# Score products of one attention layer, spread over four quarters of the array instead of two

## The chip, the core and the metric

The kernel runs on one core of a Trainium2 chip. The metric is the device time of one execution in microseconds; lower is better. The kernel before takes 2292.18 us, the median of three runs (2292.06 to 2292.21).

## What is computed

Four graph layers are applied to x, 128 graphs of 64 nodes with 256 features each. Each layer is added to its input: `x = x + layer(relu(layernorm(x)))`. Layer 0 is a graph convolution with LSTMs over windows, layer 2 a graph attention, layer 3 a filter in the eigenbasis of the graph. The change concerns the attention of layer 1, cut here to its middle part (N = 64 nodes, H = 4 heads of hd = 64 features):

```python
q = (x1 @ Wq).reshape(B, N, H, hd).transpose(0, 2, 1, 3)
k = (x1 @ Wk).reshape(B, N, H, hd).transpose(0, 2, 1, 3)
v = (x1 @ Wv).reshape(B, N, H, hd).transpose(0, 2, 1, 3)
scores = jnp.einsum('bhnd,bhmd->bhnm', q, k) / np.sqrt(hd)
scores = jnp.where(adjacency[None, None] > 0, scores, -1000000000.0)
attn = jax.nn.softmax(scores, axis=-1)
o = jnp.einsum('bhnm,bhmd->bhnd', attn, v)
o = o.transpose(0, 2, 1, 3).reshape(B, N, D)
o = o @ Wo + bo
x2 = _layernorm(x1 + o, g2, be2)
# ... the feed-forward part and a last layer norm follow
```

Everything is fp32. A graph and a head give one 64x64 score matrix, a product over 64 features.

## The kernel before

The 128 graphs are cut into 16 half groups of 8 graphs, or HT = 4 tiles of 128 rows (two graphs in a tile). `q` and `k` are kept with features on the partitions: `qT[:, m, :]` holds feature block m (128 features, so heads 2m and 2m+1, the first on partitions 0-63 and the second on partitions 64-127), and the free dimension runs over the 512 nodes of the half group. `bat(b)` is the 64 columns of graph b, `tok(t)` the 128 columns of tile t.

```python
        ps = [bank("qk") for m in range(2)]
        with plan.burst():
            for par, m, b in [(r, r ^ f, b) for f in range(2) for b in range(2 * HT) for r in (f, 1 - f)]:
                r = slice(par * N, par * N + N)
                PE.matmul(ps[m][r, bat(b)], qT[r, m, bat(b)], kT[r, m, bat(b)], start=True, stop=True)
        s = tm(4 * HT, N)
        for m in range(2):
            sm = s[:, m * 2 * HT:(m + 1) * 2 * HT, :]
            V.scalar_tensor_tensor(sm, ps[m].rearrange("p (b k) -> p b k", k=N), 0.125, vec(mask1, 2 * HT), op0=ALU.mult, op1=ALU.add)
            stat = plan.value("stat")
            softmax_shift(sm, stat[:, :2 * HT])
            ACT.activation(sm, sm, AF.Exp)
            # ... sum, reciprocal (VectorE), product with the reciprocal (GpSimd)

        pT = fm()
        for m in range(2):
            evac(pT[:, m, :], transposes([flat(s[:, (m * HT + t) * 2:(m * HT + t) * 2 + 2, :]) for t in range(HT)]), m)
        oT = fm()

        po = [bank("o") for half in range(2)]
        with plan.burst():
            for m, t, half, par in [(m, t, half, par) for m in range(2) for t in range(HT) for half in range(2) for par in range(2)]:
                r = slice(half * N, half * N + N)
                PE.matmul(po[half][par * N:par * N + N, bat(m * HT + t)], v[r, t, bat(2 * m + par)], pT[r, m, bat(2 * t + par)], start=True, stop=True)
```

The first operand of `PE.matmul` is the output in PSUM, the second the stationary operand, the third the moving one. Which partitions the operands lie on fixes the rows of the array that a product uses, and which partitions the output lies on fixes its columns. A product of 64 by 64 takes a quarter of the 128x128 array. In the score loop the output half equals the row half (`ps[m][r, ...]`, `qT[r, ...]`), and the two banks alternate from one product to the next: with f = 0 the pairs are (low rows, bank 0) and (high rows, bank 1), with f = 1 (high rows, bank 0) and (low rows, bank 1). In the second loop (attention times V, `po`) row half and output half are independent.

The instructions are not issued as they are written: a layer in the kernel records them and chooses the order on each engine beforehand from costs that it assumes. A burst counts there as one operation:

```python
    @contextmanager
    def burst(self):
        self.run, self.whole = None, True
        yield
        self.run.cost = 0.3 + 0.036 * len(self.run.calls)
        self.run.lat = self.run.cost + 0.22
        self.run, self.whole = None, False
```

All instructions are issued from one line (331), so the profile is read by operations, shapes and tile names; tile names are those of the pool buffer that happened to be free.

Of the kernel before, what the change touches and what calls it, by code (L numbers as in the profile page):

```python
# [12 lines left out]
N = 64  # L13
# [856 lines left out]
HT = 4  # L870
# [41 lines left out]
def gnn_kernel(ctx: ExitStack, tc: tile.TileContext, a, out):  # L912
# [46 lines left out]
    PE, V, ACT, G, SP = (plan.proxy(e) for e in ("PE", "V", "ACT", "G", "SP"))  # L959

    def bank(name):
        return plan.value("bank")
# [156 lines left out]
    bat = lambda b: slice(b * N, (b + 1) * N)  # L1119

    def tm(n=HT, f=D):

        return plan.value("big")[:, :n * f].rearrange("p (t f) -> p t f", f=f)

    def fm():

        return plan.value("big")[:, :2 * HT * P].rearrange("p (c n) -> p c n", c=2)
# [4 lines left out]
    def transposes(srcs):  # L1132

        pt = bank("tr")
        for i, s in enumerate(srcs):
            PE.transpose(pt[:, i * P:(i + 1) * P], s, ident)
        return pt
# [158 lines left out]
    def evac(dst, src, i):  # L1296
        if i % 2:
            ACT.copy(dst, src)
        else:
            V.tensor_copy(dst, src)  # L1300

    def to_fm(src):

        dst = fm()
        for c in range(2):
            evac(dst[:, c, :], transposes([src[:, t, tok(c)] for t in range(HT)]), 1)
        return dst

    def proj_fm(w, src, m):
        ps = bank("fm")  # L1310
        for c in range(2):
            PE.matmul(ps, w[:, c, tok(m)], src[:, c, :], start=c == 0, stop=c == 1)
        return ps

    def proj_tm(lhs, w, nk, t0):

        ps = bank("tm")
        for t in range(2):
            for c in range(nk):
                PE.matmul(ps[:, t * D:(t + 1) * D], lhs(c, t0 + t), w[:, c, :], start=c == 0, stop=c == nk - 1)  # L1320
        return ps

    def pair(t, t0):
        return flat(t[:, t0:t0 + 2, :])

    def norm(t):

        sc, bi = ln_stats(t)
        for i in range(HT):
            ACT.activation(t[:, i, :], t[:, i, :], AF.Identity, scale=sc(i), bias=bi(i))  # L1330

    def softmax_shift(s, mx):

        V.reduce_max(mx, s, axis=AX.X)
        V.tensor_sub(s, s, mx.unsqueeze(2).to_broadcast(list(s.shape)))

    def relu_norm(x):
        sc, bi = ln_stats(x)
        h = tm()
        for t in range(HT):  # L1340
            ACT.activation(h[:, t, :], x[:, t, :], AF.Relu, scale=sc(t), bias=bi(t))
        return h

    def mix_fm(h, m):

        dst = fm()
        for c in range(2):
            ps = bank("mix")
            for t in range(HT):
                PE.matmul(ps[:, tok(t)], h[:, t, tok(c)], m(t), start=True, stop=True)  # L1350
            evac(dst[:, c, :], ps, 1)
        return dst

    def layer1(x):
        h = relu_norm(x)
        lx = mix_fm(h, lambda t: lapb)
        x1 = tm()
        for t0 in (0, 2):
            ps = proj_tm(lambda c, t: lx[:, c, tok(t)], Wc, 2, t0)
            V.tensor_add(x1[:, t0:t0 + 2, :], ps.rearrange("p (t f) -> p t f", t=2), vec(bc, 2))  # L1360
        norm(x1)
        for t0 in (0, 2):
            xp, hp = x1[:, t0:t0 + 2, :], h[:, t0:t0 + 2, :]
            V.tensor_mul(xp, xp, vec(g1, 2))
            G.tensor_add(xp, xp, vec(be1, 2))
            V.scalar_tensor_tensor(xp, xp, 0.0, hp, op0=ALU.max, op1=ALU.add)
        x1T = to_fm(x1)
        qT, kT, v = fm(), fm(), tm()
        for m in range(2):
            evac(qT[:, m, :], proj_fm(Wq, x1T, m), 0)  # L1370
            evac(kT[:, m, :], proj_fm(Wk, x1T, m), 1)
        for t0 in (0, 2):
            evac(pair(v, t0), proj_tm(lambda c, t: x1T[:, c, tok(t)], Wv, 2, t0), 1)
        for t0 in (0, 2):
            G.tensor_add(x1[:, t0:t0 + 2, :], x1[:, t0:t0 + 2, :], vec(bo, 2))

        ps = [bank("qk") for m in range(2)]
        with plan.burst():  # L1380
            for par, m, b in [(r, r ^ f, b) for f in range(2) for b in range(2 * HT) for r in (f, 1 - f)]:
                r = slice(par * N, par * N + N)
                PE.matmul(ps[m][r, bat(b)], qT[r, m, bat(b)], kT[r, m, bat(b)], start=True, stop=True)
        s = tm(4 * HT, N)
        for m in range(2):
            sm = s[:, m * 2 * HT:(m + 1) * 2 * HT, :]
# [4 lines that stand above are left out]
            ssum = stat[:, 2 * HT:4 * HT]  # L1391
            V.reduce_sum(ssum, sm, axis=AX.X)
            V.reciprocal(ssum, ssum)
            G.tensor_mul(sm, sm, ssum.unsqueeze(2).to_broadcast([P, 2 * HT, N]))

        pT = fm()
        for m in range(2):
            evac(pT[:, m, :], transposes([flat(s[:, (m * HT + t) * 2:(m * HT + t) * 2 + 2, :]) for t in range(HT)]), m)
        oT = fm()

        po = [bank("o") for half in range(2)]
        with plan.burst():
            for m, t, half, par in [(m, t, half, par) for m in range(2) for t in range(HT) for half in range(2) for par in range(2)]:
                r = slice(half * N, half * N + N)
                PE.matmul(po[half][par * N:par * N + N, bat(m * HT + t)], v[r, t, bat(2 * m + par)], pT[r, m, bat(2 * t + par)], start=True, stop=True)
        for half in range(2):
            evac(oT.rearrange("p c (t b n) -> p c t b n", t=HT, b=2)[:, :, :, half, :], po[half].rearrange("p (c t n) -> p c t n", c=2, t=HT), half)
        x2 = tm()
        for t0 in (0, 2):
            ps = proj_tm(lambda c, t: oT[:, c, tok(t)], Wo, 2, t0)  # L1410
            V.tensor_add(x2[:, t0:t0 + 2, :], ps.rearrange("p (t f) -> p t f", t=2), x1[:, t0:t0 + 2, :])
        norm(x2)
        x2T = fm()
        for c in range(2):
            ACT.activation(x2T[:, c, :], transposes([x2[:, t, tok(c)] for t in range(HT)]), AF.Identity, scale=g2c[:, c:c + 1], bias=be2c[:, c:c + 1])
        V.tensor_mul(x2, x2, vec(g2))
        for t0 in (0, 2):
            G.tensor_add(x2[:, t0:t0 + 2, :], x2[:, t0:t0 + 2, :], vec(b2, 2))
        mT = [fm() for i in range(2)]
        for m in range(4):  # L1420
            ACT.activation(mT[m // 2][:, m % 2, :], proj_fm(W1, x2T, m), AF.Gelu, bias=b1[:, m:m + 1])
        for t0 in (0, 2):
            ps = proj_tm(lambda c, t: mT[c // 2][:, c % 2, tok(t)], W2, 4, t0)
            V.tensor_add(pair(x2, t0), ps, pair(x2, t0))
        for t0 in (0, 2):
            G.tensor_add(x[:, t0:t0 + 2, :], x[:, t0:t0 + 2, :], vec(be3, 2))
        norm(x2)
        for t0 in (0, 2):
            V.tensor_mul(x2[:, t0:t0 + 2, :], x2[:, t0:t0 + 2, :], vec(g3, 2))
            V.tensor_add(x[:, t0:t0 + 2, :], x[:, t0:t0 + 2, :], x2[:, t0:t0 + 2, :])  # L1430
# [55 lines left out]
    for i, g in enumerate(ORDER):  # L1486
        plan.group = REST + 2 * i
        x = X[g]
        if g < len(put):
            x = load(back[g], put[g])  # L1490
        for h in range(GT // HT):
            plan.group = REST + 2 * i + h
            xh = x[:, h * HT:(h + 1) * HT, :]
            layer1(xh)
            layer2(xh)
            layer3(xh)
            SP.dma_start(xout[g * GT // HT + h], xh)
# [54 lines left out]
```

## Time and profile before

| | before |
|---|---|
| median time | 2292.18 us (2292.06 to 2292.21) |
| span of the profiled execution | 2291.3 us |
| TensorE busy, matmul records | 2254.4 us, 11288 |
| VectorE, ScalarE, GpSimd busy | 1693.3, 969.8, 565.7 us |
| granted TensorE clock, mean | 0.996 |

In the profile PE is TensorE's products, PEld its weight loads, DVE VectorE, ACT ScalarE, POOL GpSimd. Each fp32 product leaves two matmul records. A line of the timeline merges records of the same operation that follow each other: it shows the start of the first, the time to the end of the last, and how many there are. The ends of products overlap with the next products' starts, so the distance from one line's start to the next line's start is the better measure of what a burst costs TensorE. The groups of 64x64 products all have the form 64*64 64x64, whatever buffers they use:

```profile
L331 PE MATMUL bank<-big,big 64*64 64x64 f32 x384 | 9.7, 220 | 0.0
L331 PE MATMUL bank<-big,arena 64*64 64x64 f32 x320 | 7.6, 220 | 0.0
L331 PE MATMUL bank<-x,arena 64*64 64x64 f32 x256 | 7.5, 220 | 0.0
```

These three are the largest of sixteen such groups of layer 1; the columns are count, busy time in us, mean duration of one record in ns, and idle time before.

### The profile page before, as it was taken

What the parts mean: (1) busy time and instruction counts of PE and PEld (TensorE: products, weight loads), DVE (VectorE), ACT (ScalarE), POOL (GpSimd) and SP (SyncE); (2) the same over time, 40 slices, a digit from 0 to 9 for tenths busy, and PEclk for the clock granted to TensorE, in tenths of its full rate; (3) what the DMA queues carried; (4) which work ended last, traced back from release to release, by engine and by line L of the source; (5) the groups of instructions that cost most, each with busy time, mean ns of one, the idle gap of its engine ahead of it and who ended that gap; (6) DMA issues with size and microseconds to landing.
All of it is one profiled execution on the core that took longest, in us unless ns stands there. A gap on an engine that the chain in (4) does not pass through costs nothing.

```text
span 2291.3 us, 33480 instructions
## 1 busy us (share of the span) xinstructions
PE 2254.4 (98%) x11288; PEld 1595.1 (70%) x11288; DVE 1693.3 (74%) x6942; ACT 969.8 (42%) x1909; POOL 565.7 (25%) x856
## 2 busy tenths in 40 slices
PE   8999999999999999999999999999999999999997
PEld 5578478468568568568568558778777776876786
DVE  6656666566899999999988723767786867767775
ACT  3333333333333333333333443455564545555672
POOL 3101001101100100100100203535374535555342
PEclk9999999999999999999999999999999999999998
DMA  7000001000000000000000011000000000000001
GB/s 247 1 1 19 0 1 38 19 1 1 1 1 1 1 1 1 1 1 1 5 1 1 9 36 31 1 1 10 20 10 10 10 28 10 28 10 1 2 19 37
DMA packets 27405, 35.48 MB, mean 15 GB/s; under 512 B 3297, under 2 KB 24673, under 8 KB 26721
## 3 DMA queue, kind: packets, MB, share of 16 engines
q1 hardware_dynamic: 26128, 32.29, 4.2%
q8 instruction: 89, 1.46, 0.3%
q10 hardware_dynamic: 1104, 1.05, 0.2%
q14 instruction: 84, 0.68, 0.1%
HBM read 22.85 MB, written 10.49 MB: 15 GB/s over the span
## 4 chain that ended last, share of the span: by engine, by line
PE 91%; DVE 5%; ACT 2%; POOL 1%; issue 1%; DMA 0%; SPq 0%; DVEq 0%; ACTq 0%
PE bank L331 91%; DVE arena L331 2%; DVE big L331 1%; DVE stat L331 1%; DVE x L331 1%; POOL stat L331 1%; ACT big L331 1%; DVE mids L331 0%; ACT arena L331 0%; ACT L331 0%; ACT mids L331 0%; ACT Wih L331 0%; DMA adj<-in_adj_dram 0%; ACT x L331 0%; DVE Whh L331 0%
## 5 line engine op out<-in xcount | busy, mean ns | idle before, releaser
L331 PE MATMUL bank<-big,Wih 128*128 128x512 f32 (+2 forms) x2640 | 887.6, 478 | 2.2 <-DVE arena L331 1.1
L331 PEld LDWEIGHTS bank<-big,Wih 128*128 128x128 f32 x2640 | 490.0, 190 | 275.3 <-issue 172.4
L331 ACT ACTIVATE mids<-bank,bl 128x256 f32<-128x256 f32 (+2 forms) x624 | 345.2, 563 | 637.0 <-PE bank L331 622.3
L331 PE MATMUL bank<-big,Whh 128*128 128x256 f32 (+3 forms) x1640 | 507.3, 444 | 0.0
L331 DVE TENSOR_TENSOR arena<-arena 64x21 f32<-64x21 f32 (+6 forms) x2316 | 375.9, 193 | 34.7 <-POOL arena L331 1.8
L331 PEld LDWEIGHTS bank<-big,Whh 128*128 128x128 f32 x1640 | 306.4, 190 | 132.4 <-issue 65.5
L331 POOL TENSOR_SCALAR stat<-stat 128x4 f32<-128x4 f32 (+1 forms) x228 | 67.5, 297 | 722.4 <-DVE stat L331 709.7
L331 DVE TENSOR_TENSOR big<-big,mids 128x256 f32<-128x256 f32 (+2 forms) x192 | 93.8, 489 | 123.7 <-ACT mids L331 122.3
L331 DVE TENSOR_TENSOR big<-mids 128x512 f32<-128x512 f32 (+2 forms) x256 | 145.9, 574 | 47.0 <-ACT mids L331 43.5
L331 ACT ACTIVATE mids<-big 128x256 f32<-128x256 f32 (+2 forms) x176 | 89.8, 510 | 99.6 <-DVE big L331 64.8
L331 PE MATMUL bank<-Wih,big 128*128 128x256 f32 (+1 forms) x560 | 130.2, 365 | 0.2 <-ACT big L331 0.2
L331 DVE TENSOR_SCALAR arena<-arena 64x1 f32<-64x1 f32 (+4 forms) x598 | 120.3, 210 | 8.2
L331 POOL TENSOR_TENSOR arena<-arena 64x1 f32<-64x1 f32 x66 | 43.6, 661 | 322.6 <-ACT arena L331 170.2
L331 POOL TENSOR_TENSOR stat<-stat,mhalf 128x4 f32<-128x4 f32 (+1 forms) x114 | 120.4, 1057 | 6.5
L331 PEld LDWEIGHTS bank<-Wih,big 128*128 128x128 f32 x560 | 97.6, 190 | 21.9 <-issue 10.7
L331 PE MATMUL bank<-Whh,big 128*128 128x256 f32 (+2 forms) x512 | 110.2, 358 | 1.4 <-DVE x L331 1.0
L331 ACT COPY big<-bank 128x512 f32<-128x512 f32 x113 | 63.0, 587 | 111.5 <-PE bank L331 94.1
L331 PEld LDWEIGHTS bank<-Whh,big 128*128 128x128 f32 (+1 forms) x512 | 82.3, 183 | 21.9 <-issue 8.3
L331 DVE COPY arena<-bank 64x1 f32<-64x1 f32 (+24 forms) x190 | 41.2, 220 | 71.4 <-PE bank L331 64.9
L331 PEld LDWEIGHTS bank<-adjTb,mids 128*128 128x128 f32 x512 | 69.8, 193 | 25.7 <-issue 17.0
L331 DVE BATCH_NORM_STATS2 stat<-x 128x6 f32<-128x256 f32 x240 | 87.2, 410 | 0.1
L331 ACT ACTIVATE mids<-x,stat 128x256 f32<-128x256 f32 x92 | 48.4, 591 | 88.2 <-POOL stat L331 88.2
(334 smaller groups left out, 3313.1 us busy)
## 6 DMA issues: line engine op xcount, KB each, us to landing
x<-in_x_dram SPq DMA_DIRECT2D x7, 1024.0 KB, 13.2
out_dram<-x SPq DMA_DIRECT2D x12, 512.0 KB, 2.9
Wih<-in_WihT_dram SPq DMA_DIRECT2D x3, 1024.0 KB, 15.7
Whh<-in_WhhT_dram SPq DMA_DIRECT2D x3, 1024.0 KB, 12.2
put<-x SPq DMA_DIRECT2D x2, 1024.0 KB, 4.4
arena<-put SPq DMA_DIRECT2D x2, 1024.0 KB, 5.9
out_dram<-arena SPq DMA_DIRECT2D x4, 512.0 KB, 3.0
Whh<-in_W_dram SPq DMA_DIRECT2D x2, 512.0 KB, 3.8
```

The source lines that it names most:

```text
L331: getattr(self.engines[op.eng], name)(*map(real, args), **{k: real(a) for k, a in kw.items()})
```

## The change

The heads of the second feature block (m = 1) write their scores to the other 64 partitions: output half `r ^ m` instead of `r`. With that the four products of a graph (two blocks by two heads) use each quarter of the array once, and the loop runs through them in turn. Everything behind it sees the two heads of block 1 on swapped partition halves; the attention-times-V loop undoes this by reading the other 64 columns of `pT`. The aim is that four products can be under way in the array where two were.

```diff
         ps = [bank("qk") for m in range(2)]
+        half = lambda i: slice(i * N, i * N + N)
         with plan.burst():
-            for par, m, b in [(r, r ^ f, b) for f in range(2) for b in range(2 * HT) for r in (f, 1 - f)]:
-                r = slice(par * N, par * N + N)
-                PE.matmul(ps[m][r, bat(b)], qT[r, m, bat(b)], kT[r, m, bat(b)], start=True, stop=True)
+            for b, m, r in [(b, m, r) for b in range(2 * HT) for m in range(2) for r in range(2)]:
+                PE.matmul(ps[m][half(r ^ m), bat(b)], qT[half(r), m, bat(b)], kT[half(r), m, bat(b)], start=True, stop=True)
...
-        po = [bank("o") for half in range(2)]
+        po = [bank("o") for i in range(2)]
         with plan.burst():
-            for m, t, half, par in [(m, t, half, par) for m in range(2) for t in range(HT) for half in range(2) for par in range(2)]:
-                r = slice(half * N, half * N + N)
-                PE.matmul(po[half][par * N:par * N + N, bat(m * HT + t)], v[r, t, bat(2 * m + par)], pT[r, m, bat(2 * t + par)], start=True, stop=True)
+            for m, t, i, r in [(m, t, i, r) for m in range(2) for t in range(HT) for i in range(2) for r in range(2)]:
+                PE.matmul(po[i][half(r), bat(m * HT + t)], v[half(i), t, bat(2 * m + r)], pT[half(i), m, bat(2 * t + (r ^ m))], start=True, stop=True)
```

More of the change, by code (lines that the diff above doesn't have):

```diff
@@ L1399, in layer1 @@
         oT = fm()
-        po = [bank("o") for half in range(2)]
+        po = [bank("o") for i in range(2)]
         with plan.burst():
-            for m, t, half, par in [(m, t, half, par) for m in range(2) for t in range(HT) for half in range(2) for par in range(2)]:
-                r = slice(half * N, half * N + N)
-                PE.matmul(po[half][par * N:par * N + N, bat(m * HT + t)], v[r, t, bat(2 * m + par)], pT[r, m, bat(2 * t + par)], start=True, stop=True)
-        for half in range(2):
-            evac(oT.rearrange("p c (t b n) -> p c t b n", t=HT, b=2)[:, :, :, half, :], po[half].rearrange("p (c t n) -> p c t n", c=2, t=HT), half)
+            for m, t, i, r in [(m, t, i, r) for m in range(2) for t in range(HT) for i in range(2) for r in range(2)]:
+                PE.matmul(po[i][half(r), bat(m * HT + t)], v[half(i), t, bat(2 * m + r)], pT[half(i), m, bat(2 * t + (r ^ m))], start=True, stop=True)
+        for i in range(2):
+            evac(oT.rearrange("p c (t b n) -> p c t b n", t=HT, b=2)[:, :, :, i, :], po[i].rearrange("p (c t n) -> p c t n", c=2, t=HT), i)
         x2 = tm()
```

## The prediction

> **What bounds the kernel now.** I read the busy shares first, then the engines by stage, then the waits of TensorE, then the chain that ended last, and only then single bursts on the timeline. The page's busy times:
>
> ```profile
> PE 2254.4 (98%) x11288; PEld 1595.1 (70%) x11288; DVE 1693.3 (74%) x6942; ACT 969.8 (42%) x1909; POOL 565.7 (25%) x856
> ...
> PE 91%; DVE 5%; ACT 2%; POOL 1%; issue 1%; DMA 0%; SPq 0%; DVEq 0%; ACTq 0%
> ```
>
> TensorE is busy for 98% of the span and is 91% of the chain that ended last. A busy share is an average, though, and the change touches only layer 1, so I cut the span where the first layer-1 work appears on TensorE (1437 us) and where the last half groups drain (2234 us). Columns: the stretch, then the busy time and instructions of each engine, granted clock, DMA share.
>
> ```profile
> 0.00:1437.00 1437.00, 1424.16 (x5487) 959.97 (x5488) 1073.16 (x5251) 513.58 (x1112) 152.15 (x300) 1.00 0.05 17
> 1437.00:2234.00 797.00, 788.28 (x5567) 597.64 (x5566) 590.24 (x1605) 439.92 (x766) 398.54 (x533) 1.00 0.04 12
> 2234.00:2292.00 58.00, 41.98 (x239) 37.48 (x238) 29.86 (x88) 16.30 (x32) 14.99 (x23) 0.85 0.11 37
> ```
>
> The middle stretch is the one that counts. TensorE works 788.28 of 797.00 us there and idles 797.00 - 788.28 = 8.7 us; VectorE works 590.24 us (74%), ScalarE 55%, GpSimd 50%. Time taken off TensorE here is time off the kernel, as long as the other engines hold the new pace. The first stretch has no attention. The last stretch is a drain bound by latency, and no score product falls in it: the last score burst starts at 2128.41 us.
>
> The bursts of 64x64 products are plain on the timeline of TensorE. One half group's score burst, and the next burst of attention times V (columns: start, us from first start to last end, what, count):
>
> ```profile
> 2128.41 2.08 PE L331 MATMUL bank<-mids,big 64*64 64x64 f32 x64
> 2130.42 1.13 PE L331 MATMUL bank<-Whh,arena 128*128 128x256 f32 x4
> 2131.48 1.16 PE L331 MATMUL bank<-big,x 64*64 64x64 f32 x64
> 2132.57 1.13 PE L331 MATMUL bank<-Whh,arena 128*128 128x256 f32 x4
> ```
>
> Both are 32 products in the program and 64 records in the trace (each fp32 product leaves two). From first start to the start of whatever comes next the score burst takes 2130.42 - 2128.41 = 2.01 us; the attention-times-V burst takes 2132.57 - 2131.48 = 1.09 us. Same count, same 64x64x64 shape, same type. What differs is where they sit in the array. The old score order sends its 32 products to two quarters only: rows 0-63 to output partitions 0-63, and rows 64-127 to output partitions 64-127. The attention-times-V burst walks rows 0-63 to both output halves, then rows 64-127 to both output halves: four quarters. If each quarter is a queue of its own, a score quarter holds 16 products and the other burst's holds 8; the difference of 2.01 - 1.09 = 0.92 us over 8 products is 0.115 us a product, or 0.0575 us for each of its two records. The remainder, 1.09 - 8 x 0.115 = 0.17 us, is fill and drain. So the kernel before already contains a measurement of the thing the change makes.
>
> It holds throughout: of the sixteen score bursts thirteen take 2.01 us, one (at 1614.00 us) 2.26, and two (at 1473.02 and 2017.98) run straight into the burst behind them; the attention-times-V bursts that stand alone all take 1.09.
>
> **What the Trainium skill says.** "TensorEngine Tiling (Array Packing)", section Tiling Modes, says that in 64x64 mode the array is four independent tiles that load weights and multiply in parallel, and its section Tile-to-Partition Mapping ties each to one half of the SBUF partitions it reads and one half of the PSUM partitions it writes. The trace agrees: 64 records in 1.09 us over four quarters against 2.01 us over two. The same page, section Restrictions and Gotchas (Gotcha 1: PSUM Pressure), says that different row tiles cannot access the same PSUM bank at the same time. That bears on the change directly, and no burst of the kernel before tests it at the density of the new order; I come to it as a rival. "TensorE: Matmul & The Clock Gate", Part 3, describes small products in different tiles as overlapping at a few ns from start to start; here records in different quarters start closer together than the 58 ns of a quarter, as the 64 starts inside 1.09 us show (17 ns on average).
>
> **The change part by part.** *Score burst.* It removes no product and adds none: 512 products before and after (16 half groups by 32). For the second feature block (m = 1) the output half becomes the other one, `half(r ^ m)`, so the order per batch is rows low to low, high to high, low to high, high to low: four quarters in every four products, 8 products in each. By the figures above a burst goes from 2.01 to 0.17 + 8 x 0.115 = 1.09 us. Sixteen times 0.92 us is 14.7 us of TensorE time.
>
> *Softmax.* In the second block's half of `s` the two heads have swapped partition halves. Shapes are the same, the mask is the same in both halves, so VectorE, ScalarE and GpSimd keep their work to the instruction.
>
> *Transposes and attention times V.* The transposes are untouched; the swap reappears as which 64 columns of pT are read, `2 * t + (r ^ m)`. Rows and output halves of each product are as before, in the same order, so this burst stays at 1.09 us.
>
> *Schedule.* The recording layer treats the burst as one operation whose assumed cost depends on the number of its calls, 32 in both kernels. I compared the instruction order of the two programs engine by engine: on VectorE, ScalarE, GpSimd and the DMA queue nothing differs but line numbers, and on TensorE only the order inside the sixteen bursts. Buffers and bank numbers are the same. Both banks still get their last write at the end of the burst, so a reader of the scores is released earlier only by what the burst shrinks.
>
> **How much of the 14.7 us reaches the end.** I looked up in the chain where the sixteen bursts fall. All lie in its TensorE pieces; two of these pieces, with the piece that splits them in the first case:
>
> ```profile
> 1801.37 33.07 PE bank L331 x289
> 1834.44 1.27 DVE Whh L331 x2
> ...
> 2010.45 221.35 PE bank L331 x1546
> ```
>
> The first piece ends with the burst at 1832.30, and VectorE's softmax takes the chain over at once: here an earlier burst end is an earlier softmax. The second is 221 us of TensorE with nothing else on the chain and four bursts inside (2017.98, 2055.57, 2094.28, 2128.41). To first order, then, all of it counts. But where the chain leaves TensorE for 5 to 16 us (for instance 1883.7 to 1892.4 and 1915.6 to 1931.6), a wait on another engine already bites. The waits of TensorE in the middle stretch (total us, times, longest):
>
> ```profile
> PE bank L331 <- DVE x L331: 2.1, 3, 1.0
> PE bank L331 <- ACT Wih L331: 2.0, 2, 1.5
> PE bank L331 <- ACT big L331: 1.3, 3, 0.7
> PE bank L331 <- DVE arena L331: 1.2, 1, 1.2
> ```
>
> These are nine waits of some 0.7 us on average. A burst that gives 0.92 us ahead of such a wait gives it to the wait, if what is waited for was set going before the burst. I guess that one burst in six is swallowed so, 2.5 us in all; it is a choice, supported only by these waits being few against sixteen bursts, and VectorE having a quarter of its time free. That leaves 14.7 - 2.5 = 12.2 us: 2292.18 - 12.2 = 2280.0 us, or 0.5%.
>
> **The rivals.** (a) *The bank rule bites.* In the new order two row halves write the same bank at the same moment, in different partition halves: low to low and high to high both go to bank 0. In the attention-times-V burst each bank belongs to one row half, and the old score order takes care to pair different banks, which speaks for somebody having feared this. Against it: within either partition half the new order gives bank 0 to one row half and bank 1 to the other, so the same pieces of a bank are never shared. If it did serialize, pairs would run one after the other, the burst would stay near 2.0 us and the kernel near 2292. I give this one chance in twelve. (b) *The other engines do not follow.* VectorE at 74% and the waits above could absorb half of the gain: 7 us, 2285. For it: a fixed order on every engine, so TensorE cannot slip other work into a wait. Against: 8.7 us of idle in 797 says that it hardly waits at all. One chance in six. (c) *Feeding.* TensorE's own issue might not supply four quarters; the attention-times-V burst, 64 records in 1.09 us, already shows that it does.
>
> **Range and chances.** The most that the change can give is 14.7 us, perhaps a few tenths more where a burst meets the next, so the fast end is 2277.0. The slow end, 2286.0, leaves 6 us of gain and so holds most of rival (b) but not (a). A gain over 2% would need 46 us, three times what is there, and nothing in the change adds work that could cost 46 us.
>
> **What would show it.** Right: in the changed profile each score burst is 64 records in about 1.16 us (1.09 to the next start) instead of 2.08, the 64x64 records' busy time falls by nearly 15 us, TensorE's busy time drops from 2254.4 to about 2240, the first 1437 us are unchanged, and VectorE, ScalarE and GpSimd keep their sums. TensorE's idle time in the middle stretch should grow from 8.7 to about 11 us. Wrong: bursts still near 2 us (the bank rule), or bursts at 1.1 us with idle time up by 7 us or more (the gain went into waits on VectorE or ScalarE), or an attention-times-V burst that has become longer.

## The result, and the profile after

| | before | changed |
|---|---|---|
| median | 2292.4 us (2292.06 to 2293.21, 6 runs) | 2280.94 us (2278.0 to 2281.16, 6 runs) |
| ratio | | 0.9947 (0.9934 to 0.9959) |
| TensorE busy | 2254.4 us | 2240.9 us |

The change takes 11.5 us off, half a per cent. The predicted 2280.0 us is 0.9 us away. The busy times and the chain of the changed kernel:

```profile
PE 2240.9 (98%) x11288; PEld 1581.9 (69%) x11288; DVE 1692.1 (74%) x6942; ACT 969.3 (43%) x1909; POOL 565.3 (25%) x856
...
PE 88%; DVE 7%; ACT 2%; POOL 2%; issue 1%; DMA 0%; SPq 0%; ACTq 0%; DVEq 0%
```

TensorE lost 13.5 us of busy time; VectorE, ScalarE and GpSimd kept theirs to within 1.2 us. The chain has moved a little from TensorE (91 to 88%) to VectorE (5 to 7%): the first sign that some of the gain met other engines. By stages (stretch, then busy time and instructions of each engine, granted clock, DMA share), the middle one cut where the drain begins in this kernel:

```profile
0.00:1437.00 1437.00, 1424.22 (x5485) 960.65 (x5486) 1072.67 (x5250) 512.94 (x1112) 152.09 (x300) 1.00 0.05 17
1437.00:2222.00 785.00, 774.02 (x5572) 583.45 (x5570) 590.55 (x1608) 440.05 (x766) 398.28 (x533) 1.00 0.04 12
```

The first stretch has not changed. In the middle one TensorE works 774.02 of 785 us and idles 11.0 us, against 8.7 before. The burst shown before, on the timeline of the changed kernel:

```profile
2116.26 1.16 PE L331 MATMUL bank<-mids,big 64*64 64x64 f32 x64
2117.35 1.13 PE L331 MATMUL bank<-Whh,arena 128*128 128x256 f32 x4
2118.41 1.16 PE L331 MATMUL bank<-big,x 64*64 64x64 f32 x64
```

The score burst now takes 2117.35 - 2116.26 = 1.09 us to the next start, as long as the attention-times-V burst behind it, where it took 2.01. In the trace its 64 records start in sixteen groups of four, the four within some 20 ns and 58 ns from one group to the next; in the kernel before they start in thirty-two pairs at the same distance. So four records start together where two did.

**Where the microseconds are.** I set the start of every TensorE record in one trace beside the start of the same record in the other; the order is the same outside the bursts. At the first score burst the changed kernel is 0.23 us late. At the last attention-times-V burst it is 13.07 us early (2150.21 against 2163.28). In between the difference moves in three ways. It grows by 0.92 us at each of the sixteen bursts, 14.7 us together. It shrinks at seven places where TensorE is held up longer, by 0.2 to 0.8 us, 3.1 us together. And between 1892 and 1896 us it grows by 1.7 us with no change of work, because the kernel before runs a handful of products there at half the clock and the changed kernel does not. The sum: 0.23 - 14.7 + 3.1 - 1.7 = -13.1 (the expectations below were written with 3.0 us for the waits). In the drain 1.0 us is lost again, so the span ends 12.0 us earlier.

The largest single step among the seven, on the timeline of TensorE, before and then changed. The lines are the same transposes of layer 1 (a bracket is idle time and its releaser):

```profile
1518.45 1.59 PE L331 MATMUL bank<-ident,big 128*128 128x128 f32 x12
```

```profile
1515.91 0.82 PE L331 MATMUL bank<-ident,big 128*128 128x128 f32 x6
1517.36 0.88 PE L331 MATMUL bank<-ident,big 128*128 128x128 f32 x6 [0.63 <-DVE arena L331]
```

Twelve transpose records in a row before; in the changed kernel TensorE is there 2.5 us earlier and stands still between the sixth and the seventh. The instruction of VectorE that ends this wait takes scores out of a bank:

```profile
1516.64 1.25 DVE L331 SCALAR_TENSOR_TENSOR arena<-bank,mask 128x512 f32<-128x512 f32 x2
```

In the kernel before it begins at 1518.27, so VectorE comes 1.6 us earlier where TensorE comes 2.5. Two of the sums of TensorE's waits in the middle stretch that have grown (total us, times, longest; the prediction shows 1.2 and 1.3 us for the kernel before):

```profile
PE bank L331 <- DVE arena L331: 2.0, 3, 1.2
PE bank L331 <- ACT big L331: 1.9, 5, 0.7
```

Not all seven end with VectorE. Two do (0.7 and 0.3 us are lost there); three end with ScalarE (0.8, 0.6 and 0.3 us), and at two of these three ScalarE itself had waited for GpSimd and GpSimd for VectorE; at the two smallest, 0.2 us each, no releaser shows. Of the five with a releaser one was a wait already (0.31 us before, 0.65 now); at the other four TensorE had not waited before.

The clock shows in the stages. First the kernel before, then the changed kernel, both around the same work:

```profile
1888.00:1892.00 4.00, 2.37 (x12) 1.40 (x12) 3.92 (x7) 3.93 (x7) 1.74 (x2) 1.00 0.00 0
1892.00:1896.00 4.00, 3.85 (x8) 1.57 (x7) 3.30 (x18) 2.45 (x5) 2.78 (x4) 0.57 0.02 4
```

```profile
1882.00:1886.00 4.00, 2.37 (x12) 1.42 (x12) 3.92 (x7) 3.93 (x7) 1.73 (x2) 1.00 0.00 0
1886.00:1890.00 4.00, 3.85 (x23) 2.69 (x22) 3.31 (x18) 2.74 (x6) 2.79 (x4) 1.00 0.01 4
```

After the same 4 us, in which TensorE is idle for 1.6, one kernel gets a mean clock of 0.57 and passes 8 records, the other gets 1.00 and passes 23. At the very end it is the other way round; the last eight records of TensorE, before and then changed:

```profile
2284.45 1.99 PE L331 MATMUL bank<-Wih,x 128*128 128x256 f32 x8 [0.78 <-DVE x L331]
```

```profile
2271.31 3.28 PE L331 MATMUL bank<-Wih,x 128*128 128x256 f32 x8 [0.78 <-DVE x L331]
```

The same work takes 1.3 us longer; the mean clock from 2271 to 2275 us is 0.61. The Trainium skill, "TensorE: Matmul & The Clock Gate", Part 1, describes a clock that falls to half after an idle window of some 3.4 us, the windows being free-running, so that they do not start with the kernel. The length agrees: 3.4 of 4 us at half clock give the mean of 0.57. The idleness does not: in the 3.41 us just ahead of the half clock TensorE is busy for 1.72 us, so half an idle window was enough here. Where the half clock falls differs from run to run of one kernel: the changed kernel run once more (the last experiment) has it at this work too:

```profile
1886.00:1890.00 4.00, 4.00 (x13) 2.21 (x12) 3.35 (x18) 2.50 (x5) 2.79 (x4) 0.63 0.02 4
```

The gain is not the clock's: among the runs beside that one, at an equal mean clock of 0.997, the kernel before takes 2292.0 us (mean of six) and the changed kernel 2280.0 (mean of two). The spread of the changed kernel's runs, 2278.0 to 2281.16 us, goes with the mean clock, 0.998 in the two fastest and 0.996 in the four others.

### The profile page after: what moved, and what is told of

It is laid out like the page before. It is cut to its first block, busy times and chain, and to the rows that moved or that the text cites. A ratio compares the mean times of both kernels' runs of the same rounds, so it can differ in the third digit from the quotient of the medians.

```text
span 2279.3 us, 33480 instructions
## 1 busy us (share of the span) xinstructions
PE 2240.9 (98%) x11288; PEld 1581.9 (69%) x11288; DVE 1692.1 (74%) x6942; ACT 969.3 (43%) x1909; POOL 565.3 (25%) x856
## 4 chain that ended last, share of the span: by engine, by line
PE 88%; DVE 7%; ACT 2%; POOL 2%; issue 1%; DMA 0%; SPq 0%; ACTq 0%; DVEq 0%
PE bank L331 88%; DVE arena L331 2%; DVE stat L331 2%; DVE big L331 2%; DVE x L331 1%; POOL stat L331 1%; DVE mids L331 1%; ACT big L331 1%; ACT arena L331 0%; ACT mids L331 0%; ACT L331 0%; POOL x L331 0%; ACT Wih L331 0%; DMA adj<-in_adj_dram 0%; POOL big L331 0%
```

## The experiments

My theory was that each quarter is fed on its own, a burst taking 0.17 us plus 0.115 us for each product of its fullest quarter, and that what doesn't reach the end goes into waits for VectorE. The rivals: the new loop order and not the quarters makes the gain; the array as a whole, or issue, sets the pace; two row halves in one bank cost something; the waits come from elsewhere.

### Two quarters in the new order

```diff
-                PE.matmul(ps[m][half(r ^ m), bat(b)], ...
+                PE.matmul(ps[m][half(r), bat(b)], ...
```

with `pT` read as before the change.

> The new loop order (graph, block, row half) with the old output halves: each head writes the half of its rows again, so two quarters hold 16 products each. Quarter theory (a burst takes 0.17 us plus 0.115 us for each product of the fullest quarter): 0.17 + 16 x 0.115 = 2.01 us a burst, kernel 2292 us as before. Order theory (the gain came from walking graph by graph, two products in one bank and then two in the other, and not from the number of quarters): 1.09 us a burst, kernel 2281 us.

Measured: 2292.39 us, ratio to the kernel before 0.9999 (0.9991 to 1.0008). On its timeline:

```profile
2128.35 2.08 PE L331 MATMUL bank<-mids,big 64*64 64x64 f32 x64
2130.36 1.13 PE L331 MATMUL bank<-Whh,arena 128*128 128x256 f32 x4
```

2.01 us a burst. Walking graph by graph brings nothing; it is the output half that brings the gain.

### Four quarters, block by block

```diff
-            for b, m, r in [(b, m, r) for b in range(2 * HT) for m in range(2) for r in range(2)]:
+            for b, m, r in [(b, m, r) for m in range(2) for b in range(2 * HT) for r in range(2)]:
```

> The changed kernel's four quarters, but block by block: all 16 products of block 0 (two quarters), then all 16 of block 1 (the other two). Each quarter still holds 8 products. If TensorE looks only a few products ahead, the two pairs of quarters work one after the other: about 0.17 + 16 x 0.115 = 2.01 us, at best some 0.1 less where the blocks meet, kernel 2289 to 2293 us. If it looks 16 products ahead and each quarter is fed on its own: 1.09 us a burst and 2281 us.

Measured: 2287.98 us, ratio 0.9979 (0.9971 to 0.9987).

```profile
2123.80 1.91 PE L331 MATMUL bank<-mids,big 64*64 64x64 f32 x64
2125.64 1.13 PE L331 MATMUL bank<-Whh,arena 128*128 128x256 f32 x4
```

1.84 us a burst: 16 x 0.115, the two pairs one after the other, with 0.17 us saved, which is more than the 0.1 I had allowed. In the trace the records start in pairs, as in the kernel before, except for three rounds in the middle that start in fours: some six records of block 1 run beside the last ones of block 0, and the others wait. Using four quarters is thus not enough; they must be used in turn. TensorE does not pull products of an idle quarter ahead over a run of sixteen for the busy ones. The kernel gains 4.9 us where sixteen times 0.17 is 2.8. Record by record its profiled execution is 4.8 us ahead of the kernel before at the last attention: 0.5 before the first burst, 2.8 in the bursts and 1.7 because it has no half clock in the middle stretch, less small waits. So in this pair the clock is most of the rest; its mean is 0.998 in 8 of these 14 runs, and in 3 of the 49 of the kernel before beside them.

### Block 1 twice, and all products twice

Both hold the schedule as it was (the assumed cost of the burst is kept at that of 32 calls) and issue products a second time into the same place.

```diff
-            for b, m, r in [... for r in range(2)]:
+            for b, m, r in [... for r in range(2) for again in range(1 + m)]:   # block 1 twice
+            for b, m, r in [... for r in range(2) for again in range(2)]:       # all twice
```

> The changed kernel with each product of block 1 issued twice into the same place: 48 products a burst, 8 in each of two quarters and 16 in each of the other two; the schedule is held as it was. Fullest quarter: 0.17 + 16 x 0.115 = 2.01 us a burst, kernel 2292 us. If the array as a whole sets the pace (32 products in 1.09 us over four quarters): 0.17 + 48 / 4 x 0.115 = 1.55 us a burst, kernel 2286 us.

> The changed kernel with every score product issued twice into the same place: 64 products a burst, 16 in each quarter; the schedule is held as it was. Fullest quarter: 2.01 us a burst, kernel 2292 us, the same as with block 1 alone twice and the same as before the change, with twice the products. If issue or some cost per product sets the pace of four quarters, more than 2.1 us a burst and over 2294 us.

Measured: block 1 twice 2293.22 us, ratio 1.0001 (0.9992 to 1.0009); all twice 2295.7 us, ratio 1.0013 (1.0006 to 1.002). The bursts of the two:

```profile
2128.06 2.14 PE L331 MATMUL bank<-mids,big 64*64 64x64 f32 x96
2130.13 1.13 PE L331 MATMUL bank<-Whh,arena 128*128 128x256 f32 x4
```

```profile
2131.93 2.24 PE L331 MATMUL bank<-mids,big 64*64 64x64 f32 x128
2134.09 1.13 PE L331 MATMUL bank<-Whh,arena 128*128 128x256 f32 x4
```

With 16 products in the fullest quarter a burst takes 2.01 us when it holds 32 products (the kernel before), 2.07 when it holds 48, and 2.16 when it holds 64. The fullest quarter sets the time to within that; the pace of the array as a whole, which asked for 1.55 us with 48 products, is out. It is the 48 products that decide this: with 64 an even pace of the array asks for 2.01 us too. By the marks written down beforehand (over 2.1 us and over 2294 us) the 64 came out on the side of a cost per product. That cost is small, 0.15 us for twice as many. Here two products in a row go to the same quarter, and whether that or their number costs the 0.15 us was not separated. Block 1 also has a bank of its own, so its two full quarters are one full bank, and a limit of each bank was not separated from one of each quarter. It could not explain the change itself, where each bank takes 16 products a burst in both kernels, in 2.01 and in 1.09 us.

### Banks by row half

```diff
-                PE.matmul(ps[m][half(r ^ m), bat(b)], ...
+                PE.matmul(ps[r][half(m), bat(b)], ...
...
-   ... pT[half(i), m, bat(2 * t + (r ^ m))]
+   ... pT[half(i), r, bat(2 * t + m)]
```

> The changed kernel with banks by row half: rows r write bank r, block m writes partition half m; the reads behind are adapted. No bank is written from two row halves. If two row halves in one bank (in different partition halves) cost nothing: bursts of 1.09 us and the changed kernel's 2281 us, within the spread of the clock (2278 to 2282). If they cost something: bursts below 1.09 us and a faster kernel.

Measured: 2280.65 us, ratio to before 0.9948 (0.9931 to 0.9964), where the changed kernel has 0.9947.

```profile
2118.11 1.16 PE L331 MATMUL bank<-mids,big 64*64 64x64 f32 x64
2119.20 1.13 PE L331 MATMUL bank<-Whh,arena 128*128 128x256 f32 x4
```

1.09 us: giving each bank to one row half changes nothing. In the changed kernel both row halves write a bank at once, in different partition halves, and that is free. Two row halves in the same partition half of one bank were not tried.

### Less VectorE work, before and changed

The products by the layer norm gains g1, g2, g3 of layer 1 are left out (in the inputs these are all ones), after the order has been chosen, so that each engine keeps the order of its other instructions:

```diff
-            for op in order:
+            for op in [o for o in order if not o.skip]:
...
-            V.tensor_mul(xp, xp, vec(g1, 2))
+            V.tensor_mul(xp, xp, vec(g1, 2)); plan.ops[-1].skip = True      # the same for g2, g3
```

> The kernel before without the products by the layer norm gains g1, g2 and g3 of layer 1 on VectorE (left out after the order was chosen, so every engine keeps its order); some 80 us less VectorE work. It is the base for the next run. With TensorE as the bound: 2288 to 2292 us.

> The changed kernel without the same products by g1, g2 and g3. In the full kernels TensorE gained 16 x 0.92 = 14.7 us in the bursts and gave 3.0 us of it back in waits. If those waits are on VectorE's load, they shrink with it: the last half group's attention runs 14 us or more earlier than in the light kernel before, against 13.1 between the full kernels. If the 3.0 us are lost for another reason (ScalarE, GpSimd, chance of the clock), the distance stays near 13 us or below.

Measured: 2288.98 and 2276.32 us, 12.7 us apart; ratios to the kernel before 0.9984 (0.9978 to 0.9991) and 0.9928 (0.9913 to 0.9943). VectorE's load in the middle stretch, light kernel before and then light changed kernel:

```profile
1437.00:2234.00 797.00, 787.05 (x5580) 598.75 (x5578) 534.41 (x1536) 441.76 (x769) 381.38 (x533) 1.00 0.03 12
```

```profile
1437.00:2222.00 785.00, 775.08 (x5585) 585.38 (x5583) 535.53 (x1535) 441.79 (x769) 381.03 (x533) 1.00 0.04 12
```

VectorE is at 534 us there instead of 590, and GpSimd at 381 instead of 398, so two engines are lighter, not one (VectorE by 60 us over the whole kernel, not 80). By the number written down beforehand the theory missed: the last attention runs 11.4 us earlier (2149.48 against 2160.84), not 14, which falls on the side of another reason. Record by record it looks different. The light changed kernel starts its first burst 1.27 us late, gains 16 x 0.92 = 14.7, and loses 1.7 us to a half-clock window that the other one hasn't got:

```profile
1884.50:1888.00 3.50, 3.47 (x4) 1.42 (x5) 2.98 (x17) 2.12 (x4) 1.84 (x3) 0.52 0.02 5
```

1.27 - 14.7 + 1.7 leaves 0.4 us for waits, since the sum is -11.4; the records show them at two places, 0.2 us each. In the full kernels it was 3.1 us at seven. So with the lighter engines less of the gain went into waits, as the theory asks. But this is read afterwards from one pair of traces, with the clock taken out; it points to VectorE's load and does not show it.

### The order chosen with the burst's true cost

```diff
-        self.run.cost = 0.3 + 0.036 * len(self.run.calls)
+        self.run.cost = 0.17 + 0.0288 * len(self.run.calls)    # 1.09; 0.0344 gives 1.27, 0.0228 gives 0.90
```

> The changed kernel with the burst's assumed cost set to what it takes now (0.17 + 0.0288 x 32 = 1.09 us instead of 1.45), so the order on each engine is chosen anew. If the 3.0 us of waits come from an order chosen for slower bursts: 2278 us. If not, the order is just another one: between 2276 and 2286 us.

> The kernel before with the assumed burst cost of 1.09 us, so in the same new order as the changed kernel with that cost (2274.4 us). If the new order is better by itself: 2286 to 2287 us, some 6 us below the kernel before, and the change is worth 12 to 13 us in both orders. If the new order is good only because it knows how long a score burst now takes: about 2292 us, and the change is worth up to 18 us in this order.

> The changed kernel with an assumed burst cost of 0.17 + 0.0344 x 32 = 1.27 us, halfway from 1.45 to the measured 1.09. If the nearness of the assumption to the truth is what helps: between 2274.4 and 2280.9 us, about 2278. If each order is a draw: anywhere from 2272 to 2286 us.

> The changed kernel with an assumed burst cost of 0.17 + 0.0228 x 32 = 0.90 us, below the truth by as much as 1.27 is above it. If nearness helps: about 2278 us, slower than at 1.09. If each order is a draw: anywhere from 2272 to 2286 us.

> The changed kernel once more, unaltered, on the chip of these runs, as their base: 2281 us, and as the clock windows fall 2278 to 2282.

| kernel | assumed cost | median us | ratio to before |
|---|---|---|---|
| changed | 1.09 | 2274.36 | 0.9921 (0.9906 to 0.9936) |
| before | 1.09 | 2287.76 | 0.9979 (0.9970 to 0.9988) |
| changed | 1.27 | 2277.83 | 0.9935 (0.9920 to 0.9950) |
| changed | 0.90 | 2275.47 | 0.9925 (0.9910 to 0.9940) |
| changed, again | 1.45 | 2280.11 | 0.9944 (0.9929 to 0.9959) |

The changed kernel with the order for 1.09 us is 18 us faster than the kernel before, and 5.8 us faster than with its old order. In the kernel before the order alone is worth 4.8 us (2292.59, the kernel before beside it, to 2287.76), nearer to the 6 us of an order that is better by itself than to nothing; the change in this order is worth 13.4. Part of the 4.8 is the clock: at an equal mean clock of 0.997 it is 3.5 us (2292.0 and 2288.5). In the changed kernel with that order all sixteen score bursts take 1.09 us, and TensorE's middle stretch is

```profile
1437.00:2214.00 777.00, 769.06 (x5565) 582.63 (x5564) 585.47 (x1603) 436.62 (x763) 404.25 (x533) 1.00 0.03 12
```

with 7.9 us of idle time. Set beside the kernel before in the same order, the first burst is 0.30 us late and the last 14.44 us early: 14.7 us of bursts and no net loss to waits, with nothing taken off VectorE. So the 3.1 us belonged to one order, not to the change, and VectorE's load alone does not bring them about. Why the new order is better even with the slow bursts I have not settled. The three orders don't decide between a truer cost and luck: 1.27 and 0.90 are equally far from the truth, nearness asked for about 2278 us from both, and they came out at 2277.83 and 2275.47.

## Why the prediction was right

- **The bound** was read rightly: TensorE at 98%, and 0.92 us off each of sixteen bursts reached the last attention but for 3.1 us.
- **The cost of a burst** was taken from the attention-times-V bursts of the same kernel, and 1.09 us is what came. The doubled bursts show that the formula behind it, the fullest quarter, is good to 0.15 us even with twice the products.
- **The parts said not to change** did not: the other engines' sums, the attention-times-V burst, the first 1437 us.
- **The share that is swallowed** was put at 2.5 us, one burst in six, by a guess. It was 3.1 us at seven places, and idle time in the middle stretch rose to 11.0 us where I had said about 11. The size was luck. I had looked to the nine waits that were there already, of which one grew; and most of the loss came at four places where TensorE had not waited. That VectorE or ScalarE would be what it waits for is what the traces show; that it is VectorE's load is not shown.
- **What was left out** is the clock: 1.7 us for the change in the middle and about 1 us against it at the end, in the profiled pair. The two cancel in part, so the closeness of 2280.0 to 2280.94 is partly luck; on the clock alone the changed kernel moves between 2278 and 2281.
- **The rivals:** the bank rule did not bite. The Trainium skill's sentence in "TensorEngine Tiling (Array Packing)", Restrictions and Gotchas, that different row tiles cannot access the same bank at once, goes further than what was measured: with row halves in different partition halves a burst takes 1.09 us with shared banks and 1.09 with separate ones. That the other engines do not follow came true to a fifth of the gain, and feeding was no limit.

## What to carry to other kernels

Small products that fill a quarter of the array should be dealt out to all four quarters in turn, even if a later read must undo the swap: count the products of the fullest quarter, and see that no long run of neighbours in the order goes to the same quarters (runs of two cost at most 0.15 us a burst here, a run of sixteen 0.75 us). When a kernel already has a burst of the same shape with a better layout, its time is the forecast. When a fixed order was chosen from assumed costs, put the new cost in as well and let the order be chosen again: here that gave another 6 us, though an order chosen for 0.90 us, which is not the true cost, gave 4.6.

## What I had not expected

- Block by block, four quarters were hardly better than two: 1.84 us against 2.01. A quarter that stands idle is not served ahead of a long run of products for the other ones.
- A half-clock window of 3.4 us, where TensorE has work, moves this kernel's time by 1 to 2 us, not far from the half width of the comparison's interval (2.9 us). Comparing two traces record by record separates it from the change; comparing the medians alone does not.
